# A four-layer graph stack on one core: the first pair's front computed batch by batch, the last pair's attention weights turned by TensorE

## The chip, the core and the metric

The kernel runs on one core of one Trainium2 chip. The metric is the device time of one execution in microseconds (us); for the kernel before, three runs were timed and one further execution was profiled. Five engines work in parallel, each through its own queue in order: PE (TensorE: matmuls; PEld is its weight load), DVE (VectorE), ACT (ScalarE), POOL (GpSimd) and SP (SyncE, which here only issues DMAs). An instruction that waits for another engine or for a DMA holds everything behind it in its engine's queue.

## The reference

32 batches of 512 nodes with 64 features pass through four residual layers. All layers share one 512 x 512 adjacency matrix, and before each layer comes a layer norm with a ReLU.

```
h = relu(layernorm(x)); x = x + L0(h)      # 3 steps: v = W2 relu(W1 [v, adj v] + b1) + b2; node 0 of v is set first
h = relu(layernorm(x)); x = x + L1(h)      # 2 layers: z = relu((adj z) W_i)
h = relu(layernorm(x)); x = x + L2(h)      # graph attention: 8 heads, then an output head
h = relu(layernorm(x)); x = x + L3(h)      # graph attention with additive scores

L2, each head:  hw = x W;  s = (hw hw^T) * adj;  s = -1e16 where s == 0;  out = softmax(s) hw + b
                leaky_relu (0.01) on the joined heads, an output head of the same form, leaky_relu again
L3:             h = x W;  e = leaky_relu(h a1 + (h a2)^T, 0.2) * adj (its diagonal set to 1)
                out = softmax(e) h + bias
```

Everything is float32.

## The kernel before

The 32 batches are worked on as 16 pairs. The work of a pair is cut into named jobs; "15.s1O0" is job s1O0 of pair 15. Every engine's order is the order in which the jobs stand in three lists written by hand: HEAD (the start), ROUND (a round that is repeated over the pairs, so that work of up to four pairs is interleaved) and TAIL (the end). Nothing reorders the work afterwards. PSUM has eight banks: four for scores, four ("mm") for all else; a small table, UNTIL, says for each job that takes an mm bank which later job ends its use, and a bank is given out by these places.

The jobs that matter here:

- **F0 to F32** are the front of a pair: layer norm, the three steps of layer 0, layer norm, the two layers of layer 1, layer norm (generator `front`, steps separated by `yield`; `ln_relu` is the norm, whose power of -1/2 is POOL's, L447). One of the three steps is: by-nodes matmuls (L542 or L552), their eviction, W1 on the features (L521), aggregation over the graph (L527 or L530), eviction with bias and ReLU. Layer 1 aggregates in L504. zT and zE turn the result to features, ZZ, and make a second copy with the halves swapped by two DMAs (L642).
- **k, Y** make the keys of two heads; **s** are scores (L669, with the mask L672), **r** row maxima (DVE L678), **m** negation (POOL L691), **x** exponentials with row sums (ACT L698), **n** normalising of the weights (POOL L710, reciprocal DVE L708), **t** transposing of the weights in 32 x 32 blocks (DVE L716), **v** weighing (PE L725), **us, w, y, o, c** what follows of a head (c ends with DVE L800).
- Units a, b, c, d, g, h, i, j of a pair are its eight head units, f is its output head, e its last layer. oA to oF are the norm between them.
- **weights, graph0..3, factor0..3, loops, masks, grams, vectors** prepare constants. graph transposes the adjacency (PE L358) into AT. factor prepares the second adjacency layout A2 (DVE L385), loops the third one A3. vectors prepares the last layer's weight products from w3 (64 x 64) and a12: DVE scalings of columns of a12 (L416 and two more), a PE transpose of w3 (L418), two matmuls (L421, L426) and copies (DVE L423, L424, L427).

The start of SP's queue loads x of pair 0, the adjacency A, biases, x of pair 1, the weights of layers 1 and 2, A2 (L324, 2 MB), w3 and a12 (L326, L328), the output head's weights Wo_sb (L329) and A3 (L331). In HEAD the job vectors stands just ahead of the first keys, 0.k0.

The last pair (15) is treated apart at its end, since nothing follows that could be interleaved: its output head and last layer run one batch at a time (`HalfOut`, units O0 and O1; `HalfLast`, units L0 and L1). A unit's weights are four tiles of 128 rows x 512. They are normalised by POOL and block-transposed by DVE, two tiles at a time; the values (512 nodes x 64) are spread to the layout that the block transpose asks for through DRAM (`SpreadRows`: a store, job OS or LS, and four quarters, OQ or LQ). Weighing (L1050) takes 128 matmuls of 32 x 64 weights into four banks. The sums come out as features x nodes; they are evicted with the bias (L1065, L1067), transposed back to rows of nodes (L1072), and the residual is added (L1095, L1150). Job names are s0O0, m0O0, ..., vAO0, vBO0, ouO0 (evict), otO0 (rows), orO0 (residual).

Of the kernel before, what the change touches and what calls it, by code (L numbers as in the profile page):

```python
# [14 lines left out]
P = 128  # L15
# [6 lines left out]
def gnn_stack_kernel(  # L22
# [34 lines left out]
        F3:F4 F5:F6 F7:F8 F9:F10 F11:F12 F13:F14 F15:F16 F17:F18 F22:F23 F24:F25 F26:F27 F28:F29 zT:zE k0:Y0 vA0:us0  # L57
        w00:y00 w10:y10 o0:c0 k1:Y1 vA1:us1 w01:y01 w11:y11 o1:c1 k2:Y2 vA2:us2 w02:y02 w12:y12 o2:c2 k3:Y3 vA3:us3
        w03:y03 w13:y13 o3:c3 vAE:eu et:er oT:oE oN:oV oD:oF h0:H0 h1:H1 vAL:lu lt:lr vAO0:ouO0 otO0:orO0 oT0:oE0
        oN0:oV0 vAL0:ouL0 otL0:orL0 vAO1:ouO1 otO1:orO1 oT1:oE1 oN1:oV1 vAL1:ouL1 otL1:orL1  # L60
    """
    HEAD = """
        0.weights 0.F0 0.F1 0.F2 0.biases 0.F3 0.F4 0.joined 0.F5 0.F6 1.F0 0.graph3 0.graph0 0.graph1 1.F1 0.graph2
        0.F7 0.F8 0.bjoined 0.F9 0.F10 0.F11 0.F12 0.F13 0.F14 1.F2 0.F15 0.factor0 0.masks 0.F16 0.F17 0.grams
        0.F18 0.F19 0.F20 0.F21 0.F22 0.F23 2.F0 0.F24 0.F25 1.F3 0.factor1 0.factor3 0.F26 0.F27 1.F4 0.F28 1.F5
        1.F6 0.F29 1.F7 0.loops0 0.F30 0.F31 0.loops2 0.F32 0.zT 1.F8 0.zE 1.F9 0.vectors 0.k0 1.F10 0.Y0 0.factor2
        0.ZQ03 0.ZQ12 0.k1 0.s1a 0.s0a 0.r3a 0.r2a 0.r1a 0.r0a 0.ZQ02 0.m1a 0.s3a 0.r6a 0.r7a 0.x1a 0.s2a 0.m0a
        0.r4a 0.s1b 0.r5a 0.r2b 0.m3a 0.r3b 0.m2a 0.s0b 0.x0a 0.s2b 0.nAa 0.ZQ11 0.Y1 0.ZQ01 0.x2a 0.r0b 0.x3a 0.r1b
        0.r5b 0.m1b 0.k3 0.s1c 0.r4b 0.m0b 0.x1b 0.t0a 0.s3b 0.t1a 0.nBa 0.r3c 1.F11 0.r7b 0.x0b 0.r6b 0.m3b 0.t2a
        0.m2b 0.x3b 0.nAb 0.r2c 0.s3c 0.t3a 0.x2b 0.r6c 0.m1c 0.s2c 0.ZQ13 0.r7c 0.nBb 1.F12 0.Y3 0.x1c 1.F13 0.t0b  # L70
        0.t1b 1.F14 0.k2 0.ZQ00 0.Y2 0.t3b 0.s0c 0.t2b 0.r5c 0.r0c 0.vA0 0.r4c 0.r1c 0.s3d 0.m3c 0.m0c 0.m2c 0.s0d
        0.x3c 0.vB0 0.r0d 0.vC0 0.r1d 0.x0c 0.vD0 0.nAc 0.s1d 0.t0c 0.x2c 0.r6d 0.m0d 0.r7d 0.nBc 0.t1c 0.r3d 0.s2d
        0.us0 0.w10 0.r2d 0.r5d 0.r4d 0.w00 0.m3d 0.s1g 0.m1d 0.x0d 0.x1d 0.t3c 0.m2d 0.r2g 0.y10 0.nAd 0.s3g 0.x3d
        0.r3g 1.F15 0.x2d 0.r7g 0.t2c 0.r6g 0.nBd 0.y00 0.t1d 1.F16 0.m1g 0.t0d 0.o0 1.F17 0.t2d 0.s0g 0.m3g 0.c0
        0.x3g 0.t3d 1.F18 0.loops1 0.s0h 0.x1g 0.r1h 0.r0h 1.F19 0.vA1 0.vB1 1.F20 0.r0g 0.vC1 0.m0h 0.vD1 0.s2g
        0.r1g 0.s1h 0.us1 0.r5g 0.r4g 0.m0g 0.x0g 0.w01 1.F21 0.m2g 0.nAg 0.x2g 0.y01 0.w11 0.r2h 0.r3h 0.ZQ10 0.s3h
        0.m1h 2.F1 0.s2h 1.F22 0.x0h 0.x1h 0.nBg 0.t0g 0.y11 0.r7h 0.r6h 0.s0i 0.r5h 1.F23 1.F24 0.m3h 0.r4h 0.x3h
        0.m2h 0.nAh 0.t2g 1.F25 0.s1i 0.x2h 0.t1g 0.t3g 0.r1i 0.r2i 0.o1 0.t0h 0.nBh 0.t1h 1.F26 0.s2i 0.c1 0.r0i
        0.r3i 1.F27 0.t2h 0.t3h 1.F28 1.F29 0.s3i 2.F2 0.m1i 0.vA2 0.m0i 0.r5i 0.r4i 1.F30 0.m2i 0.x0i 0.r6i 0.vB2
        0.D0 0.x2i 1.F31 0.vC2 0.vD2 0.s1j 0.r7i 0.x1i 0.r3j 0.r2j 0.us2 1.F32 0.m3i 0.s0j 1.zT 3.F0 2.F3 1.zE  # L80
        1.ZQ01 0.m1j 0.s2j 0.r1j 0.r5j 0.w12 0.r0j 0.nAi 0.m0j 0.x3i 2.F4 0.r4j 0.nBi 0.s3j 2.F5 0.r7j 0.m2j 0.r6j
        0.t0i 0.y12 2.F6 1.k0 0.t1i 1.Y0 0.w02 0.m3j 1.s1a 1.s0a 1.r2a 1.r3a 0.x0j 0.x1j 2.F7 0.t2i 0.nAj 0.x2j
        1.r0a 0.t3i 0.t0j 1.m1a 0.x3j 0.y02 1.s2a 1.ZQ02 0.nBj 2.F8 1.r1a 1.k1 1.Y1 0.t1j 0.o2 1.s3a 0.t2j 0.t3j
        0.c2 1.ZQ00 1.r6a 0.vA3 1.r7a 1.r5a 1.s1b 1.m0a 1.r4a 1.m2a 1.s0b 1.m3a 0.vB3 1.x0a 1.r2b 1.x1a 0.vC3 1.nAa
        3.F1 1.x3a 1.x2a 1.nBa 1.r3b 1.r1b 1.r0b 1.t1a 1.m1b 0.vD3 1.s3b 1.m0b 1.ZQ03 1.t0a 1.r7b 0.f0 0.us3 1.s2b
        1.x1b 1.r6b 1.r4b 2.F9 1.x0b 0.loops3 1.r5b 1.s0c 0.w03 1.r0c 1.r1c 1.m2b 1.m0c 2.F10 1.s2c 1.nAb 1.r4c
        1.x2b 0.y03 1.r5c 1.m3b 1.t2a 1.s1c 0.w13 0.y13 1.r3c 1.x3b 1.t0b 1.r2c 2.F11 0.o3 1.nBb 2.F12 1.m2c 2.F13
        1.s0d 1.s3c 1.t1b 1.m1c 1.t3a 1.t2b 0.c3 0.f1 2.F14 1.t3b 1.r1d 1.r7c 0.hQ0 1.x0c 1.vA0 1.x2c 1.ZQ12 1.r0d
        1.r6c 1.s2d 1.m3c 1.m0d 1.x1c 1.nAc 0.D1 1.s1d 1.r3d 1.r2d 3.F2 1.r4d 1.m1d 1.x0d 1.t0c 1.r5d 1.vB0 1.x1d
        1.vC0 1.nAd 1.vD0 1.us0 1.m2d 1.t1c 1.s3d 1.x3c 1.r7d 1.r6d 0.s1f 1.nBc 1.t0d 1.m3d 0.r3f 1.w10 0.r2f 1.k2  # L90
        1.y10 1.Y2 0.hQ3 0.s0f 1.w00 2.F15 1.x2d 1.x3d 1.t1d 1.t2c 1.nBd 0.r1f 1.t3c 1.y00 0.s2f 1.t2d 0.m1f 2.F16
        1.t3d 2.F17 0.hQ2 0.r4f 2.F18 1.o0 0.s3f 0.x1f 1.c0 2.F19 0.r0f 0.r6f 4.F0 0.r5f 0.r7f 1.vA1 0.m0f 1.vB1
        0.x0f 0.m2f 2.F20 1.s0g 1.ZQ13 0.hQ1 1.s2g 1.vC1 1.vD1 0.m3f 1.r0g 1.r4g 2.F21 1.s3g 0.x2f 0.nAf 1.r5g 1.m2g
        1.us1 1.r1g 1.s1g 1.w01 0.x3f 1.w11 1.y01 1.r6g 1.m0g 1.r7g 1.s0h 0.t1f 1.r2g 0.nBf 0.t0f 1.y11 1.r3g 1.x0g
        0.t2f 1.x2g 1.m1g 1.r0h 2.F22 0.t3f 1.m3g 1.x1g 1.o1 1.s1h 1.r1h 1.nAg 2.F23 1.t0g 1.x3g 2.F24 1.nBg 1.ZQ10
        1.m0h 2.F25 1.s3h 1.c1 1.r7h 1.r3h 1.x0h 0.vAE 0.vBE 0.vCE 0.vDE 1.r2h 1.s2h 0.eu 1.t1g 1.t3g 1.r6h 1.m1h
        1.t2g 1.k3 1.r4h 1.m3h 0.et 1.Y3 1.r5h 1.x1h 1.s1i 1.m2h 0.er 1.s0i 1.x2h 1.ZQ11 1.x3h 1.r2i 1.nAh 1.r1i
        1.r0i 2.F26 1.s3i 1.t0h 1.nBh 2.F27 1.r3i 1.t1h 1.s2i 1.t2h 1.r6i 2.F28 1.r4i 1.m1i 1.m0i 1.x0i 1.x1i 1.s1j
        2.F29 1.t3h 2.F30 1.r5i 1.r7i 1.vA2 1.m3i 1.r3j 1.D0 1.m2i 1.x2i 1.vB2 2.F31 1.x3i 2.F32 1.vC2 1.nBi 1.r2j
        1.vD2 1.s2j 1.m1j 1.nAi 0.oA 1.r5j 1.us2 2.zT 2.zE 1.s0j 1.r4j 1.m2j 1.s3j 3.F3 1.w12 1.x1j 1.hQ0 3.F4 1.r1j  # L100
        1.hQ1 1.r0j 1.t3i 1.y12 1.m0j 4.F1 1.r6j 1.r7j 2.k0 1.w02 1.m3j 2.Y0 1.x0j 2.s0a 3.F5 1.t2i 3.F6 1.y02 0.oB
        2.s1a 2.r1a 2.k1 2.r0a 1.x2j 1.t0i 1.nAj 2.m0a 2.s2a 2.r3a 1.x3j 2.Y1 2.r2a 2.r5a 2.r4a 2.m2a 1.nBj 3.F7
        1.t1i 3.F8 1.t0j 1.t2j 1.o2 2.s3a 1.t1j 2.s1b 1.c2 1.f0 2.m1a 1.t3j 1.vA3 2.x1a 2.x0a 1.vB3 2.x2a 2.r2b
        2.nAa 2.r6a 1.vC3 1.vD3 2.r7a 2.m3a 2.x3a 2.s0b 2.t0a 2.r3b 2.t1a 1.us3 2.nBa 3.F9 2.r1b 2.ZQ03 3.F10 2.r0b
        2.ZQ02 1.w03 2.m0b 2.s3b 1.y03
# [27 lines left out]
        12.r5g 12.r6g 10.lQ2 11.nBf 12.m3g 11.t1f 12.r4g 12.x1g 12.s0h 11.t0f 12.c1 11.t3f 11.t2f 12.m2g 12.nAg  # L133
        13.F23 12.r0h 13.F24 13.F25 12.s1h 12.x3g 12.r1h 12.m0h 12.x2g 12.r3h 12.x0h 11.vAE 12.r2h 12.m1h 12.nBg
        12.t1g 11.vBE 11.vCE 12.t0g 12.t2g 11.vDE 12.x1h 12.s2h 12.nAh 12.t3g 12.t0h 12.s3h 11.eu 12.k3 12.r4h
        12.r6h 11.et 12.Y3 12.r5h 12.s1i 12.r7h 12.m2h 12.m3h 12.t1h 12.s0i 12.r2i 12.r3i 12.m1i 12.r0i 12.x2h
        12.x3h 13.F26 13.F27 12.s2i 12.nBh 11.er 12.r1i 12.t2h 12.t3h 12.r5i 13.F28 12.r4i 12.m0i 12.s1j 14.F2
        13.F29 12.s3i 12.m2i 12.vA2 13.F30 12.D0 13.F31 12.x0i 12.r3j 12.vB2 12.vC2 12.vD2 12.x1i 12.r2j 12.x2i
        13.F32 12.us2 12.r6i 12.s3j 13.zT 12.nAi 12.r7i 12.m3i 12.m1j 14.F3 11.oA 12.s0j 13.zE 12.r7j 12.t0i 12.x3i
        14.F4 12.w12 12.r1j 12.s2j 12.y12 12.x1j 12.r6j 12.m3j 12.nBi 13.k0 12.r0j 13.ZQ03 13.Y0 12.r5j 12.w02  # L140
        13.s0a 12.r4j 12.t2i 13.s1a 12.t1i 13.r1a 13.k1 13.r0a 13.ZQ02 12.m0j 12.m2j 13.s3b 13.r2a 12.x0j 12.y02
        13.r3a 15.aO2 13.r7b 13.Y1 12.x3j 13.s3a 12.nAj 12.o2 12.x2j 13.r6b 13.r6a 13.r7a 14.F5 13.s2a 12.t3i 13.m0a
        14.F6 12.nBj 12.t0j 13.s1b 13.r4a 12.t2j 13.r3b 13.x0a 14.F7 12.t3j 13.m1a 12.c2 13.r5a 13.r2b 13.x1a 14.F8
        13.m3a 13.m2a 13.nAa 13.s0b 12.t1j 14.F9 14.F10 13.s2b 15.F0 13.x3a 13.x2a 12.vA3 13.m3b 13.m1b 13.r1b
        13.r5b 12.vB3 13.t1a 13.nBa 13.x3b 13.r0b 13.t0a 12.vC3 15.F1 12.vD3 11.oB 13.m0b 13.ZQ12 13.x1b 13.s2c
        13.ZQ01 13.r4b 13.r5c 13.s0c 12.us3 12.w03 11.oC 13.r4c 13.r1c 13.s1c 12.y03 12.w13 13.r0c 13.r3c 13.m2b
        13.x2b 13.s2d 11.oT 13.m2c 13.r2c 13.m1c 13.t3a 13.s3c 13.nBb 13.r5d 13.r4d 11.oE 12.y13 13.r6c 13.ZQ00
# [1228 lines left out]
```

## Time and profile before

| | |
|---|---|
| runs (us) | 2052.51, 2054.76 (median), 2057.88 |
| profiled execution | 2054.5 us; span 2052.6, 1.9 outside it; mean granted clock 0.992 |
| PE busy | 1998.0 us, 97% of the span |
| DVE busy | 1813.9 us, 88% |
| ACT busy | 1491.9 us, 73% |
| POOL busy | 1304.4 us, 64% |
| first scores (L669) | 65.6 us |
| last head's end (DVE L800) | 1987.0 us |

How to read it: the page gives the busy time of each engine over one execution; the trace behind it answers for any stretch. A window row lists a stretch, its length, the busy time of PE, PEld, DVE, ACT and POOL with the number of instructions, the mean clock granted to PE (1.00 is full speed), the share of DMA engines busy, and GB/s. The chain that ended last is followed back from the last instruction; "issue" is time in which an engine waited for nothing that the profile shows. In the queue of SP, L324 and so on are the lines that issue a DMA.

### The profile page before, as it was taken

The page shows a single profiled execution, that of the slowest core. Times are in us where ns is not written, and L with a number is a line of the kernel's source. Part 1 is how long each engine was busy: PE and PEld are TensorE (multiplying, and loading weights), DVE is VectorE, ACT ScalarE, POOL GpSimd, SP SyncE. Part 2 cuts the span into 40 slices and gives each one's busy share as a digit, 9 for nine tenths or more (in the row PEclk, how much of TensorE's full clock was granted, in tenths as well). Part 3 has the DMA queues.
Part 4 walks back from the last instruction along what each step waited for, and adds up shares of the span by engine and source line. Part 5 has one row for each costly group of instructions (what it writes and reads, how often), then busy time and mean ns, then how long its engine had stood idle before and what let it go on. Part 6 is the DMA issues. An engine that isn't in the chain of part 4 may idle for free.

```text
span 2052.6 us, 91028 instructions
## 1 busy us (share of the span) xinstructions
PE 1998.0 (97%) x38941; PEld 1201.2 (59%) x38941; DVE 1813.9 (88%) x4170; ACT 1491.9 (73%) x3845; POOL 1304.4 (64%) x2211
## 2 busy tenths in 40 slices
PE   6999999999999999999999999999999999999986
PEld 4556565665656566565656656566565565665555
DVE  4788889999898999989899998999999899899965
ACT  1567678777787877778777787877778687777855
POOL 3466566757667576666757567675866766566543
PEclk9999999999999999999999999999999999999997
DMA  6101111111121110212111021211111121111222
GB/s 139 33 3 35 22 31 39 36 25 37 26 41 31 36 37 19 45 25 43 29 34 38 17 45 27 43 33 31 35 23 36 27 49 33 34 30 31 41 47 65
DMA packets 257625, 74.45 MB, mean 36 GB/s; under 512 B 240324, under 2 KB 249668, under 8 KB 257220
## 3 DMA queue, kind: packets, MB, share of 16 engines
q1 hardware_dynamic: 256768, 68.54, 16.1%
q8 instruction: 305, 5.00, 1.0%
q14 instruction: 100, 0.82, 0.1%
q10 hardware_dynamic: 452, 0.10, 0.0%
HBM read 16.52 MB, written 4.78 MB: 10 GB/s over the span
## 4 chain that ended last, share of the span: by engine, by line
PE 90%; DVE 4%; ACT 2%; issue 1%; DMA 1%; POOL 1%; SPq 0%; POOLq 0%; ACTq 0%; DVEq 0%
PE s L669 23%; PE mm L725 23%; PE mm L504 6%; PE s L672 6%; PE mm L527 5%; PE mm L786 5%; PE mm L953 5%; PE mm L766 5%; PE mm L1169 3%; PE mm L530 3%; DVE sm L678 2%; PE mm L552 2%; DVE sm L716 2%; PE mm L492 1%; PE mm L521 1%
## 5 line engine op out<-in xcount | busy, mean ns | idle before, releaser
L698 ACT ACTIVATE sm<-sm,nmx 128x512 f32<-128x512 f32 x1280 | 909.6, 716 | 183.0 <-POOL nmx L691 181.4
L710 POOL TENSOR_SCALAR sm<-sm,rs 128x512 f32<-128x512 f32 x1280 | 866.2, 696 | 231.0 <-DVE rs L708 212.4
L678 DVE CUSTOM_DVE_ANT_0 sm<-s,A 128x512 f32<-128x512 f32 x1264 | 803.7, 679 | 49.7 <-PE s L672 44.0
L716 DVE STREAM_TRANSPOSE sm<-sm 128x1024 f32<-128x1024 f32 x640 | 775.4, 1229 | 52.6 <-POOL sm L710 49.8
L669 PE MATMUL s<-ZZ,Y 64*64 64x512 f32 x4096 | 553.9, 597 | 1.6 <-DVE mx L678 0.9
L725 PE MATMUL mm<-sm,vq 32*64 32x256 f32 (+1 forms) x16640 | 485.8, 376 | 2.6 <-DVE rs L708 1.8
L725 PEld LDWEIGHTS mm<-sm,vq 32*64 32x64 f32 x16640 | 384.7, 132 | 117.7 <-issue 52.5
L691 POOL TENSOR_SCALAR nmx<-mx 128x2 f32<-128x2 f32 x640 | 131.1, 216 | 361.2 <-DVE mx L678 328.9
L698 ACT ACTIVATION_READ_ACCUMULATOR sm<-sm,nmx 128x1 f32 x1280 | 246.9, 193 | 0.0
L672 PE MATMUL s<-NEGM,I2b 64*64 64x512 bf16 x2288 | 242.2, 376 | 0.0
L669 PEld LDWEIGHTS s<-ZZ,Y 64*64 64x64 f32 x4096 | 144.2, 133 | 163.4 <-issue 72.2
L778 ACT ACTIVATE y<-mm,cols 128x512 f32<-128x512 f32 x256 | 161.2, 688 | 26.3 <-PE mm L766 26.1
L672 PEld LDWEIGHTS <-I2b 64*64 64x64 bf16 x2288 | 80.2, 107 | 152.2 <-issue 150.9
L447 POOL TENSOR_TENSOR r<-ve,mhalf 128x8 f32<-128x8 f32 (+1 forms) x65 | 106.3, 1636 | 49.8 <-DVE ve L445 49.7
L766 PE MATMUL mm<-us,Wh 64*64 64x512 f32 x1024 | 133.8, 590 | 1.5 <-ACT us L760 1.4
L760 ACT COPY us<-mm 128x256 f32<-128x256 f32 x256 | 75.9, 380 | 70.0 <-PE mm L725 69.9
L786 PE MATMUL mm<-y,Wo_sb 128*64 128x256 f32 x1024 | 124.1, 384 | 2.5 <-ACT Y L1180 2.5
L504 PE MATMUL mm<-AT,z 128*128 128x512 f32 x256 | 119.9, 612 | 4.5 <-DVE z L451 4.2
L527 PE MATMUL mm<-AT,v 128*64 128x256 f32 x1024 | 117.6, 382 | 0.1
L953 PE MATMUL mm<-sm,vq 32*64 32x256 f32 x3712 | 111.8, 376 | 2.0 <-DVE rs L708 0.7
L953 PEld LDWEIGHTS mm<-sm,vq 32*64 32x64 f32 x3712 | 101.5, 132 | 15.9 <-PE s L672 7.9
L678 DVE DVE_READ_ACCUMULATOR2_ANT mx<- 128x1 f32 x1280 | 106.0, 83 | 0.0
(166 smaller groups left out, 1849.0 us busy)
## 6 DMA issues: line engine op xcount, KB each, us to landing
vq<-z SPq DMA_DIRECT2D x512, 32.0 KB
HH<-cat SPq DMA_DIRECT2D x128, 64.0 KB
vq<-catT SPq DMA_DIRECT2D x240, 32.0 KB
vq<-h3n SPq DMA_DIRECT2D x240, 32.0 KB
A<-in_adj_dram SPq DMA_DIRECT2D x5, 1024.0 KB
xt<-in_x_dram SPq DMA_DIRECT2D x32, 128.0 KB
ZZ<-ZZ SPq DMA_DIRECT2D x32, 128.0 KB
out_dram<-xo SPq DMA_DIRECT2D x32, 128.0 KB
```

Source lines behind the costliest of these rows:

```text
L504: nc.tensor.matmul(pe, lhsT=v[:, m].rearrange("p j d -> p (j d)"), rhs=AT[:, m, :], start=(m == 0), stop=(m == NT - 1),)
L527: nc.tensor.matmul(ph[out_, :], lhsT=v[:, m, j, :], rhs=AT[:, m, h], start=False, stop=stop)
L669: nc.tensor.matmul(pss[half][R[ab], :], lhsT=lhsT, rhs=rhs, start=True, stop=False)
L672: nc.tensor.matmul(pss[half][R[ab], :], lhsT=I2b[R[half], :], rhs=NEGM[R[half], k, :], start=False, stop=True)
L678: nc.vector.tensor_tensor_reduce(self.sm[:, s, :], self.pss.pop(s), self.graph(s), 1.0, -FMAX, ALU.mult, ALU.max, self.small("mx", slice(s ...
L698: nc.scalar.activation(self.sm[:, s, :], self.sm[:, s, :], AF.Exp, bias=self.small("nmx", slice(s, s + 1)), accum_out=self.small("ssum", s ...
L710: nc.gpsimd.tensor_scalar(self.sm[:, s, :], self.sm[:, s, :], self.small("rs", slice(s, s + 1)), 1.0, ALU.mult, ALU.mult)
L716: nc.vector.transpose(out=two, in_=two)
L725: nc.tensor.matmul(self.u[i][R[c], 0 : weights.shape[1] * 32], lhsT=values[32 * i : 32 * i + 32, jb, :], rhs=weights[32 * i : 32 * i + 32, ...
L766: nc.tensor.matmul(self.py[ab][c][r, :], lhsT=Wh2[R[c], self.head(c, ab), r], rhs=self.us[R[c], 2 * ab : 2 * ab + 2].rearrange("p i (s e) ...
L786: nc.tensor.matmul(self.pa[R[half], 0 : N // 2], lhsT=Wo_sb[:, self.head(k, ab), :], rhs=self.y[self.head(k, ab)][:, half * N // 2 : (half ...
L953: nc.tensor.matmul(self.u[i][r, 0 : N // 2], lhsT=values[q, jb, :], rhs=unit.sm[q, :, 32 * jb : 32 * jb + 32], start=(jb == 0), stop=(jb = ...
```

## The change

Three things, in one edit:

1. **Pair 0's front runs batch by batch.** A new generator `front_one(j)` replaces `front` and `features_of` for pair 0, with 35 steps for batch 0 (jobs A0 to A34) and 35 for batch 1 (B0 to B34). Each operation has half the size. The norm runs on DVE (with POOL's power). The last steps multiply z by the identity into both halves of the partitions, so that the features of one batch stand in both (`ZB`), and pair 0 has no ZZ and no swapping DMA.
2. **The last pair's weights are turned by PE.** In a Half unit each tile goes its own way: negation by DVE, exponentials not normalised, four PE transposes of 128 x 128 (t), a copy back to SBUF by ACT and DVE, half a tile each (e), weighing with the turned weights as lhsT and the values as rows of nodes (v: four matmuls of 64 columns), and a reciprocal and one DVE instruction that scales by the row sum and adds the bias rows or the residual. `SpreadRows` goes; two DMAs bring the bias rows. HalfOut then bends the sums (ACT) and adds the residual (DVE); HalfLast adds its bias to x3 on POOL ahead of time and sends its output in two halves.
3. **HEAD, TAIL and UNTIL are rewritten.** ROUND is the same. In HEAD the steps of A and B are interleaved; vectors stands behind 0.A8 and 0.B4 and ahead of 0.B5. In TAIL the order changes throughout; pair 15's end follows the new jobs.

```diff
     HEAD = """
-        0.weights 0.F0 0.F1 0.F2 0.biases 0.F3 0.F4 0.joined 0.F5 0.F6 1.F0 0.graph3 0.graph0 0.graph1 1.F1 0.graph2
-        0.F7 0.F8 0.bjoined 0.F9 0.F10 0.F11 0.F12 0.F13 0.F14 1.F2 0.F15 0.factor0 0.masks 0.F16 0.F17 0.grams
-        0.F18 0.F19 0.F20 0.F21 0.F22 0.F23 2.F0 0.F24 0.F25 1.F3 0.factor1 0.factor3 0.F26 0.F27 1.F4 0.F28 1.F5
-        1.F6 0.F29 1.F7 0.loops0 0.F30 0.F31 0.loops2 0.F32 0.zT 1.F8 0.zE 1.F9 0.vectors 0.k0 1.F10 0.Y0 0.factor2
...
+        0.A0 0.A1 0.B0 0.B1 0.A2 0.weights 0.A3 0.biases 0.joined 0.A4 1.F0 0.A5 0.B2 0.bjoined 0.A6 0.graph1
+        0.graph2 0.graph3 0.graph0 0.B3 0.masks 0.A7 0.A8 0.B4 0.vectors 0.B5 0.B6 1.F1 0.B7 0.B8 0.A9 0.A10 0.B9
+        0.A11 1.F2 0.B10 0.B11 0.A12 0.factor1 0.A13 0.A14 0.B12 0.A15 0.B13 0.factor0 0.A16 0.factor3 0.A17 0.B14
+        0.B15 0.A18 0.B16 0.A19 0.grams 0.B17 0.A20 0.A21 0.A22 0.A23 0.A24 0.B18 2.F0 0.B19 0.A25 1.F3 0.B20 0.A26
+        0.A27 0.A28 0.factor2 0.B21 0.A29 1.F4 0.A30 0.A31 0.B22 0.B23 0.B24 0.B25 0.B26 0.A32 0.B27 0.A33 0.B28
+        0.A34 0.B29 0.k0 1.F5 0.B30 0.Y0 0.s1a 0.s0a 1.F6 0.B31 0.r3a 0.r2a 0.k1 0.s1b 0.r0a 0.r1a 0.s2a 0.m1a 0.B32
...
+    def front_one(j):
+        s = state[0]
+        x = xts[0][:, :, j, :]
+        v = yield from ln_relu(x, True)
...
+        for step in range(STEPS):
+            k = min(step, 1)
+            pvs = by_nodes_one(hT, lambda r, k=k: W1T[r, 1, k, r])
+            yield
+            v = bp.tile([P, NT, D], F32, tag="b", name="v")
...
+            ph = mm_ps()[:, : N // 2]
+            for r in R:
+                nc.tensor.matmul(ph[r, :], lhsT=W1T[r, 0, k, r], rhs=hT[r, :], start=True, stop=False)
+            aggregated_one(v, ph, False)
+            yield
+            hT = bp.tile([P, N // 2], F32, tag="b", name="hT0")
+            nc.scalar.activation(hT, ph, AF.Relu, bias=b1k[k])
+            yield
...
+        pts = [mm_ps() for _ in R]
+        for t in range(NT):
+            for pt, a in zip(pts, R):
+                for r in R:
+                    nc.tensor.matmul(pt[r, hblk(t)], lhsT=z[a, t, :], rhs=ident[a, a], start=True, stop=True)
+        yield
+        s["ZB", j] = bp.tile([P, N], F32, tag="b", name="ZB")
+        joined_halves(s["ZB", j], pts, True)
...
     def batch(p, j, half):
+        if p == 0:
+            return state[p]["ZB", j][R[half]]
         return state[p]["ZZ"][int(half != j)][R[half]]
...
-        def weigh(self, part):
-            if part == 0:
-                self.u = [mm_ps() for _ in range(4)]
-            values = spread[self.p, self.kind, self.j].tile
-            for jb in range(part * JB // 2, (part + 1) * JB // 2):
-                for i in range(4):
-                    q = slice(32 * i, 32 * i + 32)
-                    nc.tensor.matmul(
-                        self.u[i][R[0], 0:P],
-                        lhsT=values[q, jb, :],
-                        rhs=self.sm[q, :, 32 * jb : 32 * jb + 32],
...
+        def turn(self, t):
+            pw = self.pws[t] = mm_ps()
+            for m in range(NT):
+                nc.tensor.transpose(pw[:, blk(m)], self.sm[:, t, blk(m)], ident)
+
+        def turned_kept(self, t):
+            pw = self.pws.pop(t)
+            nc.scalar.copy(self.sm[:, t, half[0]], pw[:, half[0]])
+            nc.vector.tensor_copy(self.sm[:, t, half[1]], pw[:, half[1]])
+
+        def weigh(self, t):
...
+            values = state[self.p][self.values_of, self.j]
+            for m in range(NT):
+                nc.tensor.matmul(
+                    self.pns[t // 2][:, hblk(t)],
+                    lhsT=self.sm[:, t, blk(m)],
+                    rhs=values[:, m, :],
...
+        def divided(self, t, to, plus):
+            one = slice(t, t + 1)
+            nc.vector.reciprocal(self.small("rs", one), self.small("ssum", one))
+            nc.vector.scalar_tensor_tensor(
+                to, self.pns[t // 2][:, hblk(t)], self.small("rs", one), plus, ALU.mult, ALU.add
+            )
...
+            self.divided(t, self.xo[:, t, :], s["x3", self.j][:, t, :])
+            if t % 2:
+                two = slice(t - 1, t + 1)
+                nc.sync.dma_start(
+                    out=out[2 * self.p + self.j].rearrange("(t q) d -> q t d", q=P)[:, two], in_=self.xo[:, two]
+                )
```

## The prediction

> **What bounds the kernel now.** I read the page's busy shares first, then PE's busy time in chosen windows, then the start of SP's queue, then the chain at the end.
>
> ```profile
> span 2052.6 us, 91028 instructions
> PE 1998.0 (97%) x38941; PEld 1201.2 (59%) x38941; DVE 1813.9 (88%) x4170; ACT 1491.9 (73%) x3845; POOL 1304.4 (64%) x2211
> ```
>
> PE idles 54.6 us of the span. The windows (stretch, its length, then busy time of PE, PEld, DVE, ACT, POOL, granted clock, DMA share, GB/s) say where:
>
> ```profile
> 20.40:30.00 9.60, 9.31 (x126) 6.46 (x124) 2.97 (x10) 1.47 (x3) 3.72 (x3) 1.00 0.95 169
> 40.20:43.60 3.40, 3.20 (x4) 1.50 (x5) 0.05 (x1) 0.00 (x0) 0.00 (x0) 0.50 0.69 108
> 46.00:65.50 19.50, 15.85 (x274) 9.91 (x277) 14.18 (x28) 3.87 (x12) 7.63 (x11) 0.96 0.10 22
> 85.00:95.00 10.00, 8.50 (x156) 4.41 (x148) 8.33 (x17) 7.29 (x19) 3.85 (x9) 1.00 0.05 10
> 105.00:200.00 95.00, 95.00 (x1716) 55.14 (x1712) 82.05 (x190) 65.12 (x169) 62.55 (x108) 1.00 0.08 17
> 1987.40:2052.60 65.20, 41.94 (x882) 33.65 (x882) 35.38 (x91) 31.30 (x79) 17.94 (x32) 0.80 0.29 65
> ```
>
> Between 105 and 200 PE has no gap. So a shorter front is worth only the PE idle it removes, and PE work that it leaves undone is paid later in full. The end, from the last head's cat (DVE L800) at 1987.0, idles PE for 23.3 us at a clock of 0.80.
>
> Before 30 the DMA decides. SP's queue and its waits (us in total, times, longest):
>
> ```profile
> 13.51 1.47 SPq L324 DMA_DIRECT2D A<-in_adj_dram  x2
> 15.08 0.92 SPq L326 DMA_DIRECT2D early<-in_L_gnn_weight_dram  x1
> 17.96 1.76 SPq L328 DMA_DIRECT2D a<-in_L_gnn_a_dram  x2
> ```
>
> ```profile
> SPq L329 <- DMA A<-in_adj_dram: 5.9, 1, 5.9
> SPq L331 <- DMA A<-in_adj_dram: 3.9, 1, 3.9
> ```
>
> A2 (2 MB) goes out at 13.51; w3 and a12, a few KB, are issued behind it at 15.1 to 18.0. DMA traffic of 23 to 24, then of 30 to 31:
>
> ```profile
> DMA packets 104, 0.20 MB, mean 205 GB/s; under 512 B 4, under 2 KB 4, under 8 KB 104
> DMA packets 20, 0.00 MB, mean 5 GB/s; under 512 B 20, under 2 KB 20, under 8 KB 20
> ```
>
> Up to 25 nearly all packets are A2's long rows. The small ones run from 25 to 31, and none is left from 31 on: w3 and a12 are there at about 30.8, hidden today because vectors, which needs them, is run at 60.8.
>
> The end of the chain:
>
> ```profile
> 2032.00 4.57 issue
> 2036.57 5.67 PE mm L1050 x109
> 2044.28 3.83 issue
> 2048.11 0.61 DVE yT L1065 x2
> 2049.32 0.42 DVE xo L1150
> ```
>
> The last exponential ends at 2037.3; normalising, block transposes, two weighings, evictions, rows and the output DMA (2.85 from 2049.74) take 15.3 more.
>
> **Head: the steps by batch.** A pair's step takes 5.1 to 5.3 us now (L542 at 22.33, L552 at 27.41, L542 at 32.67). A half-size step has half the matmul records (L527, 32 in 3.67: 1.84) and shorter evictions (DVE .42); with its by-nodes matmuls and semaphores I get 3.6 to 3.8. The total PE work is equal, plus about 0.65 for features turned to both halves; two SP issues of 1.16 us and their flight go.
>
> **Head: vectors moved.** It now stands right behind A7, A8 and B4, about 39 instructions into PE's order. Aggregation A7 should end at 21.9: the adjacency's copies are done at 19.7 and eight matmuls follow. PE's transpose L418 then waits for w3, DVE's L416 for a12, until 30.8, and both queues are in order: behind them stand B5, B7, A9, A11, the whole chain. That is 8.9 us in which PE does 8.6 us of work today. DMA order is unchanged, so I see nothing that moves w3 up.
>
> After it, a granted clock of about 0.5 for one stretch: in 40.20 to 43.60, after PE's gap, the trace shows 0.50, and L504's eight matmuls of 40.4 take 5.25 instead of 3.67. The Trainium skill, "TensorE: Matmul & The Clock Gate", Part 1, states that one idle window of about 3.4 us halves the clock until a busy window has passed, which speaks against this edit. By that rule alone the cost would be an estimated 1.7 us. I use the row's own difference, 1.6.
>
> The chain by hand: B5 32.7 (half clock), B7 35.7, A9/A10 36.6, A11 38.9, B11 41.1, step 3 44.2, x1 45.5, its normalisation 49.7 (half-size DVE pieces .4 to .17 and POOL's power 1.03, about 4 in all), two layers of 3.0 to 3.2 to 55.9, normalisation 59.7, features 60.8, keys and first scores 2.8: **63.6**, against 65.6 today. From stall to scores that is 32.8 us where the pair takes 43.2 from the same point (22.33).
>
> But 5.3 us of PE work done by 65.6 today is still owed then (1.F7 4.3, 1.F9 .65, the rest of B). So head: −2.0 + 5.3 = +3.3; less PE's idle in the ramp (85 to 95: 1.5), which owed work and B's features fill: **+1.7**. Without the stall the scores come at 47 to 53 and the sum turns to −6 to −10.
>
> **End: weights turned on PE.** Per unit (four units, four tiles each):
>
> - Gone: POOL's normalise, 4 x .69; DVE's block transposes, 2 x 1.23; weighing L1050, 128 records in 3.46 to 4.24; L1072 .45; five DMAs with the spread (store to last quarter about 3).
> - Added on PE: four turns a tile. L358 (128x128, float32) ran 16 in 2.93: .73 a tile. Weighing, four matmuls a tile: the nearest row is L1117, 64 rows x 128 columns with 66 values out, 8 in 1.10, or .53 for four; that has half the rows and runs back to back. L375 at .42 each gives 1.7 a tile; L376 at .28 gives 1.1. I take 1.05, ends .53 and 1.7. PE gains 2.5 to 3.5 a unit, 10 to 14 in all, into its 23.3 of idle.
> - Added elsewhere: per tile an ACT copy .37 and a DVE copy .42, one behind the other; DVE negate .15, reciprocal .13, scaling with the addition about .25; ACT bend .24.
>
> Times from the last cat (0 = 1987.0): turns and weighing of O0 until 8.3; scores O1 8.3 to 12.9 (today 5.65 to 10.8: PE's extra work stands before them); O1's exponentials 12 to 17; pair 14's last scores 17.3 to 26.4; O1's normalisation from 28.3 (today 25.6); oT1 42.3 (today 41.7); scores L1 46.6 (today 45.0); exponentials until 53.0 (today 50.3); last turn 53.8; copies 55.4; weighing until 58.0, scaling 58.5, output 2.85: **61.35 against 65.6, −4.25**. The later exponentials cost +2.65, the shorter way out gives −6.9 (8.4 for 15.3). Moving 15.s1O0 behind 15.vD3 fills PE's gap of 1.36 at 1981.84: −1.35. **End −5.6.** Bounds: weighing at 1.7 a tile, four tiles on the path, +2.6; another half-clock stretch +1.6 as in L504's row; at .53 a tile −2.1, and −2 if O1's scores slip less.
>
> In between the repeated order is unchanged and PE is full. In the reordered stretch 1850 to 1987 PE idles 6.4 us: ±2.
>
> **Sum.** +1.7 − 5.6 = −3.9 on an execution of 2054.5 (span 2052.6 and 1.9 around it): 2050.6. That execution lies 0.3 below the median of the runs shown, 2054.76. I say **2050**.
>
> **Rivals.** 0.3% is 6.2 us, about what a measurement of this kernel can tell from no change.
>
> 1. *The stall is cheap or absent* (w3 sooner, or PE's missed work fits into gaps). For: 8 to 9 us of DMA wait depends on the position of a few small packets. Against: SP's waits above. Head −2 to −10, end −5.6: 2039 to 2047, half of it beyond −6.2 together with the better end. Also here: the forecast's head with an end of −8 to −10.
> 2. *The stall decides; slower.* Place: PE's L418 at 21.9. If two batches on the same in-order queues take as long per step as the pair, the lag of 8.5 us (30.8 for 22.33) is never made up: first scores at 74. Head +8.5 + 5.3 − 1.6 = +12.2; with the end −5.6 to −1 it gives 2061 to 2066. It decides from first scores at about 73.5. For: DVE and ACT serve both batches in order, and DVE, also blocked by L416, has the factors behind it (L385, 1.61 each). Against: today PE idles 9.2 us between 30 and 65.5, waiting for the chain.
> 3. *The end gives nothing*: PE's extra 10 to 14 us lands on the path, since 0 to 13 is PE's own chain. Then 2054 to 2061.
>
> **Chances.** The forecast, 2044 to 2054: .42 (of it .17 beyond −6.2). Rival 1: .28, all counted faster. Rival 2: .22. Rival 3: .08, no change. So faster .45, no change .33, slower .22. The range 2038 to 2063 leaves out the lower tail of rival 1 (.06) and the upper half of rival 2 (.13).
>
> **What would show it.** Right: in the profile after, a PE gap of 8 to 9 us from about 22 ending at w3's landing, half a clock behind it, first scores at 61 to 66; at the end about 61 us from the last cat, the 16 turns of a unit near 2.9 us. Wrong: no gap at L418; scores before 55 (rival 1) or after 72 (rival 2); weighing over 1.7 a tile; an end over 65.

## The result, and the profile after

The changed kernel takes 2046.99 us (median of 6 runs) against 2054.4 (6 runs): ratio 0.9964, 95% interval 0.9952 to 0.9976, so 7.4 us less. The profiled execution took 2046.44 us, its span 2044.7 against 2052.6. That is 0.36%, a little more than the 0.3% that the prediction took as its bound, with an interval that reaches to either side of it.

```profile
span 2044.7 us, 90579 instructions
PE 1998.0 (98%) x38701; PEld 1196.2 (59%) x38701; DVE 1818.6 (89%) x4247; ACT 1497.2 (73%) x3866; POOL 1289.9 (63%) x2193
```

PE's busy time is the same to a tenth; what went is idle time. The windows (same columns as in the prediction) say where:

```profile
20.40:30.00 9.60, 4.02 (x40) 2.20 (x36) 1.92 (x6) 1.07 (x3) 0.00 (x0) 0.91 0.99 175
30.00:40.40 10.40, 10.21 (x105) 5.62 (x107) 4.18 (x13) 1.73 (x4) 3.92 (x3) 0.75 1.03 206
46.00:65.50 19.50, 15.49 (x290) 10.23 (x290) 12.96 (x35) 4.62 (x12) 6.29 (x5) 1.00 0.04 8
85.00:95.00 10.00, 9.65 (x128) 6.22 (x128) 10.00 (x19) 7.53 (x20) 8.16 (x19) 1.00 0.25 55
105.00:200.00 95.00, 95.00 (x1680) 53.53 (x1676) 82.01 (x185) 66.48 (x171) 64.01 (x111) 1.00 0.07 14
1987.10:2044.70 57.60, 43.99 (x546) 34.70 (x545) 39.74 (x139) 35.66 (x97) 10.15 (x16) 0.83 0.17 38
```

The stall is in the first two rows: PE is busy 4.02 of 9.60 us where it had been busy 9.31, and then works at a mean clock of 0.75. In the last row the end has 44.0 us of PE work in 57.6 us, where the prediction's row had 41.9 in 65.2. PE's timeline around the stall and at the first scores (start, duration, engine, line, operation, what it writes and reads, count, idle time ahead of it and its releaser; L427 of the changed file is the transpose of w3, L418 before):

```profile
28.58 0.45 PE L427 MATMUL mm<-ident,early 128*128 128x128 f32 x1 [5.04 <-DMA early<-in_L_gnn_weight_dram]
29.57 0.56 PE L430 MATMUL mm<-a,w3T 128*128 128x4 f32 x2 [0.54 <-DVE w3T L428]
32.18 3.38 PE L654 MATMUL mm<-AT,v 128*64 128x256 f32 x16
36.96 1.95 PE L654 MATMUL mm<-AT,v 128*64 128x256 f32 x16
66.29 1.09 PE L777 MATMUL s<-ZB,Y 64*64 64x512 f32 x8 [0.27 <-ACT Y L1305]
```

PE waits 5.04 us for the load of w3. Sixteen aggregation records take 3.38 at 32.2 and 1.95 at 37.0. Behind the wait the granted clock is 0.50 from 28.30 to 35.12 and 1.00 after that:

```profile
28.30:35.12 6.82, 6.00 (x39) 3.55 (x41) 2.71 (x11) 0.27 (x1) 2.26 (x2) 0.50 0.92 209
```

First scores come at 66.3, against 65.6.

Where the whole difference lies is best read from one instruction that occurs 32 times, DVE's completion of a batch's cat (L800 before, L908 after). From the trace, end of that instruction:

| end of cat | before | after | difference |
|---|---|---|---|
| 6th of 32 | 435.39 | 437.06 | +1.67 |
| 16th | 1040.86 | 1042.50 | +1.64 |
| 24th | 1525.97 | 1527.37 | +1.40 |
| 32nd, the last | 1987.43 | 1987.51 | +0.08 |
| from there to the end | 65.16 | 57.14 | −8.02 |

So in these two executions the head costs 1.6 us, the stretch between the 16th and the last cat gives 1.5 back (1.3 of it behind the 24th, in the new order of TAIL), and the end after the last cat is the gain. PE in that end:

```profile
1987.60 1.09 PE L1152 MATMUL mm<-ident,sm 128*128 128x128 f32 x8
1990.15 2.89 PE L1165 MATMUL mm<-hn,sm 128*128 128x64 f32 x24
2020.07 6.21 PE L833 MATMUL mm<-sm,vq 32*64 32x128 f32 x248 [1.97 <-DVE sm L824]
2036.14 1.65 PE L1152 MATMUL mm<-ident,sm 128*128 128x128 f32 x12
2037.63 3.68 PE L1165 MATMUL mm<-h3n,sm 128*128 128x64 f32 x32
```

A tile's turn is four records of L1152, .55 us; its weighing is eight records of L1165 (two for each matmul), .92 to .98. L833 is pair 14's last weighing; note its 6.2 us.

### The profile page after: what moved, and what is told of

It reads as the page before. It is cut to its first block, busy times and chain, and to the rows that moved or that the text cites. A ratio compares the mean times of both kernels' runs of the same rounds, so it can differ in the third digit from the quotient of the medians.

```text
span 2044.7 us, 90579 instructions
## 1 busy us (share of the span) xinstructions
PE 1998.0 (98%) x38701; PEld 1196.2 (59%) x38701; DVE 1818.6 (89%) x4247; ACT 1497.2 (73%) x3866; POOL 1289.9 (63%) x2193
## 4 chain that ended last, share of the span: by engine, by line
PE 91%; DVE 4%; ACT 2%; POOL 1%; DMA 1%; issue 1%; SPq 0%; ACTq 0%; POOLq 0%; DVEq 0%
PE s L777 24%; PE mm L833 23%; PE s L780 6%; PE mm L894 5%; PE mm L536 5%; PE mm L874 5%; PE mm L1061 5%; PE mm L513 5%; PE mm L1294 3%; PE mm L539 2%; DVE sm L786 2%; PE mm L561 2%; DVE sm L824 2%; PE mm L501 1%; PE mm L530 1%
## 5 line engine op out<-in xcount | busy, mean ns | idle before, releaser
L806 ACT ACTIVATE sm<-sm,nmx 128x512 f32<-128x512 f32 x1264 | 898.3, 717 | 162.6 <-POOL nmx L799 161.0
L818 POOL TENSOR_SCALAR sm<-sm,rs 128x512 f32<-128x512 f32 x1264 | 852.3, 693 | 223.4 <-DVE rs L816 193.3
L824 DVE STREAM_TRANSPOSE sm<-sm 128x1024 f32<-128x1024 f32 x632 | 765.3, 1229 | 52.5 <-POOL sm L818 49.6
L777 PE MATMUL s<-ZZ,Y 64*64 64x512 f32 x3840 | 510.8, 596 | 1.1 <-ACT Y L1305 0.9
L833 PE MATMUL mm<-sm,vq 32*64 32x256 f32 (+1 forms) x16640 | 484.0, 377 | 5.7 <-DVE sm L824 5.3
L833 PEld LDWEIGHTS mm<-sm,vq 32*64 32x64 f32 x16640 | 382.1, 132 | 120.6 <-issue 49.3
L780 PE MATMUL s<-NEGM,I2b 64*64 64x512 bf16 x2288 | 237.1, 377 | 0.0
L777 PEld LDWEIGHTS s<-ZZ,Y 64*64 64x64 f32 x3840 | 131.3, 133 | 144.7 <-issue 64.8
L513 PE MATMUL mm<-AT,z 128*128 128x512 f32 x240 | 111.0, 605 | 0.1
L536 PE MATMUL mm<-AT,v 128*64 128x256 f32 x960 | 110.2, 382 | 0.0
```

The lines of the kernel that those rows point to most:

```text
L513: nc.tensor.matmul(pe, lhsT=v[:, m].rearrange("p j d -> p (j d)"), rhs=AT[:, m, :], start=(m == 0), stop=(m == NT - 1),)
L536: nc.tensor.matmul(ph[out_, :], lhsT=v[:, m, j, :], rhs=AT[:, m, h], start=False, stop=stop)
L777: nc.tensor.matmul(pss[half][R[ab], :], lhsT=lhsT, rhs=rhs, start=True, stop=False)
L780: nc.tensor.matmul(pss[half][R[ab], :], lhsT=I2b[R[half], :], rhs=NEGM[R[half], k, :], start=False, stop=True)
L806: nc.scalar.activation(self.sm[:, s, :], self.sm[:, s, :], AF.Exp, bias=self.small("nmx", slice(s, s + 1)), accum_out=self.small("ssum", s ...
L818: nc.gpsimd.tensor_scalar(self.sm[:, s, :], self.sm[:, s, :], self.small("rs", slice(s, s + 1)), 1.0, ALU.mult, ALU.mult)
```

## The experiments

**Head and end apart.** Two mixtures of the two files: `end_only` has the old front and HEAD with the new end and TAIL, `front_only` the reverse.

```diff
 end_only:    + Half/HalfOut/HalfLast, half_jobs, bias rows and TAIL of after;  front, batch, HEAD of before
 front_only:  + front_one, batch, HEAD of after;  Half classes, SpreadRows, TAIL of before
```

> Pair 0's front and HEAD as before the change; the last pair's end, TAIL and its classes as after. Theory (the end is the whole gain, the head a small loss): the last head's cat comes at about 1985.5 (1987.1 of the changed kernel less its lag of 1.6), the way from it to the end takes 57.6 again, total about 9.5 us below the kernel before (ratio 0.9954). Rival (the batch-wise head is part of the gain): 5 us or less below the kernel before.

> Pair 0's front by batch and the new HEAD; the last pair's end, TAIL and its classes as before the change. Theory: every head after round one lies 1.6 us later than before and the end is unchanged: about 1.6 us above the kernel before (ratio 1.0008). Rival: the lag is lost in the stretch from 1850 on, where PE has gaps, and the time is the same within 0.5 us; or the head gains, 2 us or more below.

`end_only`: 2047.3 us, ratio 0.9961 (0.9949 to 0.9974). `front_only`: 2057.94 us, ratio 1.0018 (1.0009 to 1.0027). From the last cat to the end it is 57.50 and 65.93 us: the end's 8 us come with the new end alone, its way of turning and its order of jobs together; no run parts the two. The head alone is a loss of 3.8 us, 1.8 to 5.5 by the interval; expected was 1.6. `end_only` was expected at about 9.5 us below the kernel before and is 6.8: together with the new end, the loss of the head does not show (2047.3 without it, 2047.0 with it). The trace gives the same picture: the last cat ends at 1987.35 in `end_only`, 1987.51 after, 1988.66 in `front_only`, although in the rounds they lie 0.6, 1.6 and 2.3 us behind the kernel before. From the 24th cat to the last, the kernels with the new TAIL gain 0.3 (`end_only`) to 1.3 us (the changed kernel) on the kernel before, `front_only` with the old TAIL 0.2; why the gain differs so much is not shown. Effects below one microsecond can't be told apart here; `end_only`, whose front is the old one, has its first scores at 67.1 in its profiled execution and the kernel before at 65.6.

**The stall taken away, in two ways.** `vectors_late` moves the job, `small_first` moves the loads.

```diff
 vectors_late:
-        ... 0.A8 0.B4 0.vectors 0.B5 ... 0.A19 0.grams 0.B17 ...
+        ... 0.A8 0.B4 0.B5 ... 0.A19 0.grams 0.vectors 0.B17 ...
 small_first:
-    for r in R:
-        nc.sync.dma_start(out=A2[r], ...)
     for j, r in enumerate(R):
         nc.sync.dma_start(out=w3bd[r, r], in_=w3)
         ...
+    for r in R:
+        nc.sync.dma_start(out=A2[r], ...)
```

> The changed kernel with one job moved: vectors goes from behind B4 to behind grams (ahead of B17), some 25 us later. Theory (PE and DVE stand still at vectors until w3 lands): the gap of 5.0 us at 23.5 and the half clock behind it are gone, first scores 6 to 8 us sooner (58 to 60 instead of 66.3), all later heads 6 to 8 sooner, total about 2040. Rival (the chain is bound elsewhere): DVE meets the factors' wait for A2 instead, or the chain's own latency shows, and the gain is under 3 us.

> The changed kernel with the loads of w3 and a12 issued ahead of A2 instead of behind it; vectors stays where it is. Theory (the place in the DMA queue is the stall): the small loads land near 18 to 20, no gap at vectors, A2 lands 4 to 5 us later (SP's issue time), first scores 5 to 7 us sooner, total about 2041. Rival: the delayed A2 stops DVE at factor1 or delays w3 all the same, and the gain is under 2 us.

`small_first`: 2041.6 us, ratio 0.9936 (0.9924 to 0.9949), 5.4 below the changed kernel. Its window from 20 to 66, and PE's only wait at vectors:

```profile
20.00:66.00 46.00, 40.36 (x608) 23.57 (x606) 29.50 (x79) 12.78 (x32) 11.77 (x11) 1.00 0.52 102
25.44 0.36 PE L430 MATMUL mm<-a,w3T 128*128 128x4 f32 x2 [0.54 <-ACT hT L669]
```

The gap at vectors is .54 us, there is no half clock before 66, and first scores come at 60.5 instead of 66.3. At the 6th cat it is 5.8 us sooner than the changed kernel and 4.2 sooner than the kernel before, at the 24th 5.2 and 3.8. So the place of a few small packets in the queue cost 5 to 6 us.

`vectors_late`: 2044.99 us, ratio 0.9954 (0.9941 to 0.9966): 2 us, less than expected, though the stall at 23.5 is gone. First scores came at 65.4. Its DVE timeline, and its window from 46 to 56, show what took the gain:

```profile
42.15 0.42 DVE L425 TENSOR_SCALAR w3T<-early,a 128x64 f32<-128x64 f32 x2 [2.77 <-DMA xt<-in_x_dram]
```

```profile
46.00:56.00 10.00, 8.85 (x80) 5.01 (x80) 6.59 (x14) 0.75 (x3) 4.27 (x3) 0.50 0.01 2
```

DVE's first instruction of vectors waits 2.77 us. The DMA named there is not the cause: this instruction waits on several semaphores, among them PE's, and it starts when grams' matmuls on PE end (42.04). Vectors' w3T and grams' turned weights share one buffer. Batch 0's norm stands behind it on DVE, PE runs dry, and the whole of 46 to 56 goes at half clock. A third place tests that reading:

```diff
-        ... 0.A8 0.B4 0.vectors 0.B5 ... 0.A18 0.B16 0.A19 0.grams ...
+        ... 0.A8 0.B4 0.B5 ... 0.A18 0.B16 0.vectors 0.A19 0.grams ...
```

> The changed kernel with vectors moved to just ahead of 0.A19 and grams. In vectors_late it stood behind grams: grams' turned weights and vectors' w3T share one buffer, so DVE's first instruction of vectors waited 2.8 us for grams' matmuls, with the norm of batch 0 behind it on DVE, and a half clock of 10 us followed. Theory (place in DVE's queue, not the move itself, took that gain): here DVE waits for nothing, no half clock before the first scores, first scores at 60 to 62, total 2041 to 2043, like small_first. Rival (the loads' order is what small_first gained, not the place of vectors): 2045 or more, like vectors_late.

The same window of `vectors_mid`:

```profile
46.00:56.00 10.00, 7.18 (x126) 4.33 (x122) 8.06 (x20) 2.12 (x7) 4.97 (x4) 1.00 0.01 2
```

`vectors_mid`: 2044.23 us, against 2055.91 for the kernel before in the same series: ratio 0.9940 (0.9927 to 0.9954). The absolute time is above the expected 2041 to 2043, and the interval of the ratio reaches both that of `small_first` and that of `vectors_late`, so the total does not decide between theory and rival. The trace does: first scores at 61.1 against 65.4 in `vectors_late`, full clock in the window above, and at the 6th cat 4.2 us between the two (2.3 at the last cat). That DVE waits for nothing did not come true: it waits 1.75 us for PE's transpose of w3 instead of 2.77 for grams, and batch 0's normalised z comes only 1.0 us sooner (44.94 against 45.93). So most of the difference at first scores goes with the half clock that did not follow. Two jobs' distance in a list decided that.

**PE's price in the end.** Each turn of one unit is issued three times, into the same place:

```diff
+            for again in range(3 if (self.kind, self.j) == ("O", 0) else 1):   # ("L", 1) in l1_turn_x3
                 for m in range(NT):
                     nc.tensor.transpose(pw[:, blk(m)], self.sm[:, t, blk(m)], ident)
```

> The changed kernel with each of unit O0's 16 PE transposes issued three times into the same place (the same values): 32 more matmuls, 8 tiles' turns at .55 to .6 us, 4.4 to 4.7 us of PE work right behind the last cat and ahead of O1's scores. Theory (the prediction's step: PE's own chain sets the start of O1, and a slip there passes on to the end): the changed kernel's time plus 3 to 4.5 us, about 2051. Rival (pair 14's last layer on ACT, POOL and DVE sets the middle of the end, and O1 has slack): plus 1 us or less.

> The changed kernel with each of unit L1's 16 PE transposes issued three times into the same place: the same 4.4 to 4.7 us of PE work in the last unit. Theory (of the last unit all PE work from its first ready tile is on the path, because PE is busy without a gap there): plus 3 to 4.5 us, about 2050.5. Rival (three of the four tiles hide behind the exponentials): plus 1.2 us, the extra turns of the last tile alone.

PE's timeline of `o0_turn_x3`, the turns of O0:

```profile
1989.94 5.46 PE L1153 MATMUL mm<-ident,sm 128*128 128x128 f32 x48
```

`o0_turn_x3`: 2051.8 us, ratio 0.9982 (0.9973 to 0.9991). O0's turns end 2.8 us later after their start than in the changed kernel (5.46 against 2.63 with its wait of .45), and from the last cat to the end it is 60.17 against 57.14: +3.03. `l1_turn_x3`: 2051.22 us, ratio 0.9984 (0.9975 to 0.9992); 8 extra turns at .455 are 3.6 us, from the last cat to the end 60.49: +3.35. PE's work counts about one for one at both places (3.03 for 2.83, 3.35 for 3.64); the rivals (slack in O1, cover by the exponentials) are out. The extra work was smaller than expected, since back to back a turn is .455 us. The medians rose by 4.8 and 4.2; the 1 to 2 us beyond the end's +3 lie ahead of the last cat (1989.85 and 1988.32), in code that was not touched. Most of them are there at first scores, 67.98 and 67.22 against 66.29, and 1.4 and 1.0 us of them by the end of the stall:

```profile
29.94 0.30 PE L427 MATMUL mm<-ident,early 128*128 128x128 f32 x1 [4.58 <-DMA early<-in_L_gnn_weight_dram]
```

This is `o0_turn_x3`; in `l1_turn_x3`, `warm_end` and `front_only`, which have the same head, the same record starts at 29.55, 29.55 and 29.80, in the changed kernel's profile at 28.58. That profile is the quickest of the five. Why the load of w3 comes at different times is not shown.

**The half clock in the end.** In the changed kernel, most of 2010 to 2026.5 runs at half clock, as its window says:

```profile
2010.00:2026.50 16.50, 10.96 (x268) 8.52 (x268) 13.63 (x35) 9.25 (x23) 7.98 (x12) 0.54 0.06 15
```

```diff
+    def kept_busy(bank, times):
+        for _ in range(times):
+            nc.tensor.matmul(bank, lhsT=ident, rhs=AT[:, 0, :], start=True, stop=True)
 # 1 ahead of 15.oT0's transposes, 1 ahead of 15.de0's matmuls, 5 ahead of 14.vAL's, each into the bank written next
```

> The changed kernel with seven matmuls (identity by AT, 128 x 128 by 512, their result overwritten) put where PE waits in the end: one ahead of 15.oT0's transposes, one ahead of 15.de0, five ahead of 14.vAL; .92 us each at full clock by L504's row before. Theory (the half clock from 22 to 39 us after the last cat comes from PE's waits, and half of vL's 6.2 us is due to it): no half clock in that stretch, vL in 3.5 to 4 us, total 2 to 3 us below the changed kernel, about 2044.5. Rival 1 (vL is bound by its weight loads and not by the clock): no gain within 0.5 us. Rival 2 (the clock stays at half all the same): the seven matmuls take 1.8 us each and add 2 to 5 us.

> The kernel small_first with the same seven matmuls in its end. Theory: the gains add up, about 2039 (2041.6 less 2 to 3). Rival: as for the seven matmuls on the changed kernel, no gain or a loss.

The same window of `warm_end`, and pair 14's weighing in its timeline:

```profile
2010.00:2026.50 16.50, 12.72 (x289) 7.79 (x288) 15.13 (x41) 11.58 (x32) 8.20 (x13) 1.00 0.09 20
```

```profile
2021.60 3.78 PE L835 MATMUL mm<-sm,vq 32*64 32x128 f32 x248 [2.23 <-DVE sm L824]
```

`warm_end`: 2045.88 us, ratio 0.9956 (0.9944 to 0.9969). The clock is full, pair 14's weighing takes 3.78 instead of 6.21 us, and from the last cat to the end it is 55.03 against 57.14: −2.1. The median fell by 1.1 only, less than the expected 2 to 3: this execution's last cat came at 1989.05, 1.5 later than in the changed kernel, in code that is the same (its first scores came at 67.4, 1.1 later). `small_first_warm`: 2038.26 us (4 runs), ratio 0.9918 (0.9905 to 0.9932), 3.3 below `small_first`; from the last cat 54.84 against 57.09. The two gains add up, and this version beats both kernels: 16 us below the kernel before, 8.7 below the change.

## Why the prediction was right, and where its steps were off

The direction, the forecast case and the range held: 2050 was said, 2046.99 measured, in 2038 to 2063. The sum was −3.9; in the profiled executions it is −7.9 of the span, and nearly all of the difference is in the end. By its own steps:

**The head's sum, +1.7, is the +1.6 of the rounds, by luck: two of its terms were off and cancel, and in the other four profiles with this head the 6th cat lies 2.4 to 3.4 us behind the kernel before.** (The prediction's own terms, −2.0 + 5.3 − 1.5, give 1.8.) The stall is there, behind the same job and for the same load, but it is 5.0 us and not 8.9. It begins later (23.5 for 21.9; PE had waited 2.2 us at 17.4 for DVE, among the adjacency's transposes, which the chain by hand left out), and A2 lands sooner, as SP's waits show:

```profile
SPq L340 <- DMA A<-in_adj_dram: 4.4, 1, 4.4
SPq L338 <- DMA A<-in_adj_dram: 3.5, 1, 3.5
```

They add up to 7.9 us; before, the same two waits were 9.8. The half clock behind the stall then lasted 6.8 us, where the prediction counted one stretch like the 3.4 us of its row, and the two layers of batch 0, with pieces of batch 1 between them, brought its features at 63.8 instead of 60.8. So first scores came 2.7 us later than the chain by hand had them. The owed work less the ramp was put at +3.7 and is +0.9 (1.6 less the 0.7 by which first scores are late): PE's idle time between 66 and 105 fell from 1.5 to 0.6, and the half clock of 64 to 67.5, 3.4 us in the kernel before, is gone; the sum had not credited that. No run separates these terms.

**The end, −4.25 from the last cat: it is −8.0.** The way out from the last exponential is 57.55 − 49.1 = 8.45 us where 8.4 was forecast for 15.3. In its pieces there is luck: the last turns end 1.6 us after that exponential and not 0.8, the weighing of four tiles ends 3.5 us behind them, and the copies, put at 1.6 ahead of 2.6 of weighing, are covered. The term that failed is the slip of +2.65 ahead of it: the last exponential came 1.2 us sooner than before. After the last cat's start, forecast and measured:

| | before | forecast | after |
|---|---|---|---|
| O0 weighed | 5.1 | 8.3 | 7.2 |
| scores O1 done, with masks | 11.2 | 12.9 | 11.7 |
| O1's exponentials done | 14.1 | 17 | 15.2 |
| pair 14's last scores done | 20.7 | 26.4 | 23.2 |
| O1's norm starts | 26.0 | 28.3 | 25.0 |
| oT1 | 41.7 | 42.3 | 39.6 |
| scores L1 done | 45.0 | 46.6 | 43.1 |
| last exponential done | 50.3 | 53.0 | 49.1 |
| end | 65.6 | 61.35 | 57.55 |

(The prediction read 10.8 and 25.6 in the second and fifth row of the kernel before: without the last masks, and at the addition ahead of the norm.) Weighing had the right price (1.05 taken, .92 to 1.0 measured), the turns had not: .73 taken from L358, whose records took .183 each at the start; those of the end took .136 in O0 and .114 back to back, .55 and .455 a tile. Why the start's are dearer no run shows. That is 1.1 us with the weighing at O0, which `o0_turn_x3` shows to pass on to the end about one for one. Another 1.4 is pair 14's scores on ACT, done in 8.0 us after O1's exponentials and not in 9.4; the rest are tenths at each step. The larger estimate was made by adding PE's extra work to the old order of jobs, and it left out what O1's norm had waited for there:

```profile
2004.61 6.32 PE L1050 MATMUL mm<-sm,vq 32*64 32x128 f32 x128 [6.43 <-DMA vq<-h3n]
```

PE stood 6.43 us ahead of O1's weighing, which needs the block-transposed weights and the values spread through DRAM; it then took 6.32 and ended 23.9 us after the last cat; in the changed kernel it ends at 20.1, and pair 14's scores come last, at 23.2. The extra PE work itself was put at 10 to 14 us and is about 3: turns and weighing take 25.2 us in this end, where weighing and rows took 22.1. The prediction priced each old weighing at 3.46 to 4.24 us, but two of the four took 6.32 and 5.76: the granted clock was 0.50 from 2002.8 to 2009.7 and from 2033.6 to 2040.4.

**The filled gap of 1.36 at 1981.8**: the gap is gone, but PE's idle time between 1850 and 1987 rose from 5.95 to 7.63 us. The rise is between 1900 and 1950, 1.62 to 4.24, and it brings a half clock that the kernel before does not have (before, then after):

```profile
1909.04:1915.87 6.83, 6.83 (x200) 4.98 (x186) 5.58 (x19) 6.31 (x12) 0.60 (x3) 1.00 0.28 51
1909.04:1915.87 6.83, 6.04 (x32) 2.36 (x26) 6.72 (x21) 6.69 (x16) 0.93 (x5) 0.50 0.22 47
```

Every kernel with the new TAIL shows 6.8 us of it, beginning between 1904 and 1912; the two with the old one do not. No run filled this gap or moved 15.s1O0 alone, so this term stays open.

**The rivals.** The first (stall cheap or absent) is half true: 5 us instead of 8.9, and its price without the stall, 6 to 10 us below the kernel before for the head, is 4.2 in `small_first`. The second, where the lag is never made up, did not come: from the stall's end (28.6) to first scores batch 0 needs 37.7 us, against 43.2 for the pair and 32.8 forecast. Its ground was real, as `front_only` shows: this head alone is slower. The third (the end gives nothing) is out.

The Trainium skill, "TensorE: Matmul & The Clock Gate", Part 1, names one idle window of about 3.4 us as what halves the clock. At the stall this case agrees: PE idled 5.0 us, and 0.50 followed. In the end the half clock came without such a window: it began at 2008.0, behind a stretch in which PE worked 2.13 of 3.41 us and waited 0.5 and 0.8, as the changed kernel's windows show. There the measurement decides.

```profile
2004.62:2008.03 3.41, 2.13 (x18) 1.78 (x18) 3.12 (x12) 3.41 (x8) 1.08 (x3) 1.00 0.28 58
2008.03:2025.10 17.07, 10.78 (x215) 8.05 (x220) 15.56 (x42) 10.91 (x29) 8.19 (x13) 0.50 0.09 22
```

That half clock vanished where `warm_end` filled the gaps, which was worth about 2 us. What the 6.8 us of half clock behind the stall cost, no run separates from the stall.

## What to carry to other kernels

When a job is moved forward in an in-order queue, ask when its inputs land and who else holds its buffers, then ask what stands behind it on each engine it uses; here one job's place was worth 5 us at the first scores, and the cure was to issue a few small loads ahead of a large one. Compare two long schedules by one instruction that recurs in both: the offset tells head, middle and end apart before any explanation. Where an end runs with gaps, look at the granted clock of the stretch on the critical chain: a few idle matmuls in the gaps bought about 2 us.

## What the runs showed of the hardware that was not expected

A run of short gaps is enough for a long half-clock stretch: in the end of the changed kernel the clock was 0.50 for 17.07 us. It began behind waits of 0.5 and 0.8 us, and further waits of 1.3, 3.0 and 2.0, with work between them, fell inside it. A weighing of 248 records of 32 rows x 64 columns by 128 took 6.21 us there and 3.78 in `warm_end`; but only its first 5.03 us were at half clock (the row's records are counted in both stretches where they overlap the edge):

```profile
2020.07:2025.10 5.03, 5.03 (x191) 5.03 (x196) 0.50 0.02 7
2025.10:2026.28 1.18, 1.18 (x73) 0.93 (x57) 1.00 0.00 0
```

Its records started 26.3 ns apart at half clock and 15.9 after it, 14.2 in `warm_end`: a factor of 1.7 to 1.9. And the same front code reached its last cat up to 2.3 us apart in different profiled executions, which is as much as some of the terms of the prediction; 1.0 to 1.4 of that was there when w3 had landed.
